# A graph layer with residual and norm on one core: x's three bf16 parts taken from its bytes, tables ahead of the edges' work, one set's picks by another queue

## The chip, the core and the metric

The kernel runs on one core of a Trainium2 chip: TensorE (PE) with its weight loads (PEld), VectorE (DVE), ScalarE (ACT), GpSimd (POOL), SyncE (SP), and sixteen DMA engines that they share. Each engine works through its own instructions in order; SP, ACT and POOL also issue DMAs from their queues. The metric is the device time of one execution in microseconds.

## The reference

Inputs are x (12500 x 128, float32), 400000 edges with source, target (sorted by target) and a type 0 or 1, and three 128 x 128 weights with biases.

```python
Xs = X[src]
m_data = Xs @ W_data.T + b_data
m_ctrl = Xs @ W_control.T + b_control
msg = jnp.where((edge_types == 0)[:, None], m_data, m_ctrl)
agg = jax.ops.segment_sum(msg, dst, num_segments=X.shape[0])
out = jax.nn.relu(agg + (X @ W_self.T + b_self))
x = _layernorm(x + out, axis=-1)          # mean and variance over the row, eps 1e-5
```

## The kernel before

**What is summed.** The kernel does not multiply each edge by a weight. It sums source rows per target and type, and multiplies the sums afterwards. The edges are cut into 25 groups of 125 columns of 128 edges. Of each group about a fifth comes by gathers from DRAM (`p`, GpSimd's indirect DMAs at L754) and the rest is picked from x in SBUF by TensorE (`e`, 107 sets of 20 columns, L820). Since TensorE works in bf16, x is held as three bf16 parts whose sum is x: `x3` in SBUF with 98 blocks of 128 rows, and `rows3`, the same in DRAM, for the gathers.

**The split of x** (`split_x`, L245). x is cut into eight pieces: six of 14 blocks, one of 13 and one of a single block with 84 rows. Four float32 tiles `xt` hold fetched pieces; a unit splits a piece and then issues the fetch of the piece four later into the tile that comes free (ACT's queue, L257). The split alternates two engines: ScalarE rounds x to bf16 (L262), VectorE subtracts it (L263), ScalarE rounds the rest (L264), VectorE subtracts that (L265). `store_rows` (L269) writes each piece's parts to `rows3` from SP's queue.

**A set of picked edges** (`give_slots`, L546). Each edge has a block of x (its source over 128) and a lane in it. Every one of 100 cells (blocks, two of them spare) has room for 32 edges of a set; VectorE and TensorE work out each edge's rank in its cell: `O` compares blocks with cells (L504), `prod` and `ahead` count (L576, L594, L598, L603 to L607), `eq` finds equal blocks in one lane (L565), `rm` and `rv` lay rank, lane and code out (L504, L635; `placed[0]` is the rv written down last). TensorE collects them (L647), ScalarE copies them to `cell` (L655), and two DMAs by SP's queue bring the lanes to all partitions: `there` in DRAM (L657) and from there `pick`, 800 KB (L659). VectorE compares `pick` with the partition's number (L690), and from then on TensorE can pick the set's rows out of `x3` (L820). ScalarE copies them to bf16 (`emsg`, L834), and TensorE adds them up with a 0/1 matrix of targets (`esel`, L504; L704 and L842). Edges beyond 32 in a cell are fetched by a spare gather (`last`, L798), used at the end of the set. `accumulate` adds the sums to `acc` (L743); finished rows are multiplied by the weights, added to x and normed.

**The opening.** Before the first set, the kernel loads the edges of group 0 and the first targets of all windows, makes tables (comparison columns, identity, `ltri`) from GpSimd's iotas (L304 to L345), works out each window's first node (`halves`, `node0`, L357 to L368), prepares group 0's edges (`prep_e`, L475: relative targets, codes, and copies of blocks, lanes and codes by ScalarE), splits x, ranks sets 0 and 1, and finds the windows' places (`places_and_weights`, L374, written down behind the third piece of x). Lines 1029 to 1047 give that order.

**What sets the order.** The instructions are written down in one order; for every engine a planner at build time makes a list from that order and its own estimate of when inputs are there. `merged` and `evenly` interleave units of work by a share of the set, and `paced` ties gathers to a point of TensorE's work. `tc.issue_after(ins)` queues the instructions of its block that run on `ins`'s engine behind `ins` on that engine; work of other engines in the block is not touched by it.

Of the kernel before, what the change touches and what calls it, by code (L numbers as in the profile page):

```python
# [10 lines left out]
I32 = mybir.dt.int32  # L11
AF = mybir.ActivationFunctionType
# [138 lines left out]
def short_path(ctx, tc, const, ident, eps, wT, brow, bad, x, src, dst, etype, ws, bs, out):  # L151
# [93 lines left out]
    def split_x(pool):  # L245
# [13 lines left out]
        def split(b, m, rows):  # L259
            t = tiles.pop(b)  # L260
            h, mm, lo = (x3[:rows, b:b + m, j, :] for j in range(3))
            nc.scalar.copy(h, t)  # L262
            nc.vector.tensor_sub(t, t, h)  # L263
            nc.scalar.copy(mm, t)  # L264
            parted.append(nc.vector.tensor_sub(lo, t, mm))  # L265
# [10 lines left out]
        for k, p in enumerate(pieces):  # L276
            def unit(k=k, p=p):
                split(*p)
                if k + ahead < len(pieces):
                    fetch(*pieces[k + ahead])  # L280
# [63 lines left out]
    for a in range(4):  # L344
        nc.vector.tensor_scalar(ltri[:, a, :], free[:, a, :], own_f[:, a:a + 1], None, op0=OP.is_gt)  # L345
# [10 lines left out]

    halves = tmp.tile([1, 2, NG * NE], I32, name="halves")  # L357
    nc.vector.memset(x3[:, NBLK - 1], 0.0)
    first = first_i["e"].rearrange("o g w -> o (g w)")
    nc.vector.tensor_single_scalar(halves[:, 0, :], first, 7, op=OP.logical_shift_right)  # L360
    nc.vector.tensor_single_scalar(halves[:, 1, :], first, 127, op=OP.bitwise_and)
# [12 lines left out]
    def places_and_weights():  # L374
        near = raw["near"] = keep.tile([rows_p, NG], FP, name="near")
        from_i = tmp.tile([rows_p, 1], I32, name="from_i")
        from_f = tmp.tile([rows_p, 1], FP, name="from_f")
        nc.gpsimd.iota(from_i, pattern=[[0, 1]], base=-PAD, channel_multiplier=DPC)
        nc.vector.tensor_copy(from_f, from_i)
        for k in range(1, NE):  # L380
            ge = raw[f"ge{k}"] = tmp.tile([rows_p, 1], FP, name=f"ge{k}")
            nc.vector.tensor_scalar(
                ge, from_f, float(DPC * PB * k - PAD), float(-DPC * PB), op0=OP.is_ge, op1=OP.mult
            )
        for k in range(1, NE):
            nc.vector.tensor_add(from_f, from_f, raw.pop(f"ge{k}"))
# [5 lines left out]
        least = tmp.tile([1, NG, NWIN], FP, name="least")  # L392
        for i, (_, _, c, _) in enumerate(windows(0)):
            nc.vector.memset(least[:, :, i:i + 1], float(max(0, c * DPC - PAD)))
# [80 lines left out]
    def prep_e(g):  # L475
# [17 lines left out]
        for v, val in enumerate((parts[:, 1, :], code)):  # L493
            nc.scalar.copy(vals2[:, :, v, :], val.rearrange("p (n o) -> p n o", o=1).to_broadcast([P, n, 2]))
# [551 lines left out]
    for u in prep_p(0):  # L1046
        u()
# [201 lines left out]
```

## Time and profile before

Three runs took 1756.07, 1758.43 and 1759.98 us; the median is 1758.43. The profiled execution took 1757.87 us, and its span, from the first instruction to the last, is 1756.1 us.

| stretch, us | length | PE busy | DVE busy | ACT busy | POOL busy | GB/s |
|---|---|---|---|---|---|---|
| 0 to 68 | 68 | 5.72 | 55.42 | 27.34 | 3.67 | 257 |
| 68 to 1700 | 1632 | 1563.90 | 1513.37 | 1169.52 | 1295.19 | 147 |
| 1700 to 1757 | 57 | 45.66 | 26.45 | 32.38 | 17.78 | 59 |

"Busy" leaves out waits and DMA issues. An engine's row in the profile names the line, the engine, the operation, what it writes from what it reads, how often, and in brackets how long the engine stood idle before it and what ended that wait. The mean granted clock of TensorE is 0.995.

### The profile page before, as it was taken

How to read it: one execution, taken by the hardware profiler on the slowest of the kernel's cores; microseconds unless marked ns; L12 is line 12 of the kernel's file. 1: busy time of each engine (PE TensorE's matmuls, PEld its weight loads, DVE VectorE, ACT ScalarE, POOL GpSimd, SP SyncE). 2: the span in 40 equal slices, each digit the busy share in tenths (PEclk: the TensorE clock that was granted, in tenths of full speed). 3: DMA queues.
4: the chain of work that ended last, by engine and by line, in shares of the span. 5: the costliest groups of instructions: out<-in, count | busy, mean ns of one | idle time of the engine just before them, and what ended most of it. 6: DMA issues, size and time to landing. Idle time of an engine off the chain costs nothing.

```text
span 1756.1 us, 72083 instructions
## 1 busy us (share of the span) xinstructions
PE 1615.3 (92%) x29945; PEld 1311.7 (75%) x29945; DVE 1595.2 (91%) x3996; ACT 1229.2 (70%) x2249; POOL 1316.6 (75%) x1109
## 2 busy tenths in 40 slices
PE   0599999999999999999999999999999989999997
PEld 0377777777778777777877877777777777878786
DVE  8899999998999998999988999999999989999993
ACT  4577777767677667767766777776777766767675
POOL 0288877787777787877887877887877877777871
PEclk9999999999999999999999999999999999999999
DMA  8655454446454545444535454544454535544441
GB/s 237 209 165 160 128 158 136 147 125 199 115 164 134 159 125 179 143 152 127 166 119 164 150 164 133 164 122 147 160 159 135 158 108 162 167 139 141 151 139 41
DMA packets 190562, 261.28 MB, mean 149 GB/s; under 512 B 86437, under 2 KB 155983, under 8 KB 187152
## 3 DMA queue, kind: packets, MB, share of 16 engines
q1 hardware_dynamic: 126894, 148.02, 25.9%
q0 software_dynamic: 50704, 102.16, 20.8%
q10 hardware_dynamic: 12626, 6.40, 1.2%
q8 instruction: 236, 3.87, 0.9%
q14 instruction: 102, 0.84, 0.1%
HBM read 238.47 MB, written 18.00 MB: 146 GB/s over the span
## 4 chain that ended last, share of the span: by engine, by line
PE 48%; DVE 32%; issue 6%; DMA 6%; ACT 5%; DVEq 1%; POOL 1%; SPq 0%; POOLq 0%; ACTq 0%
PE sums L704 22%; PE got L820 15%; DVE esel L504 3%; PE side L950 3%; DVE pick L690 3%; PE sums L842 3%; DMA last<-rows,idx 3%; DVE rv L635 2%; ACT emsg L834 2%; DVE prod L598 2%; DVE prod L576 2%; PE side L584 2%; DVE acc L743 2%; PE side L647 2%; DVE ahead L594 2%
## 5 line engine op out<-in xcount | busy, mean ns | idle before, releaser
L754 POOL DMA_INDIRECT msg<-rows,pidx x985 | 1190.9, 1209 | 307.5 <-issue 118.9
L834 ACT CAST emsg<-got 128x768 bf16<-128x768 f32 (+1 forms) x1070 | 951.9, 930 | 303.9 <-PE got L820 289.8
L704 PE MATMUL sums<-esel,emsg 128*128 128x176 bf16 x7704 | 683.4, 240 | 0.0
L704 PEld LDWEIGHTS <-emsg 128*128 128x128 bf16 x7704 | 566.9, 98 | 68.7 <-issue 28.5
L820 PE MATMUL got<-x,pick 128*32 128x384 bf16 x10486 | 568.0, 330 | 21.9 <-DVE pick L690 14.7
L820 PEld LDWEIGHTS <-pick 128*32 128x32 bf16 x10486 | 239.2, 96 | 139.2 <-issue 20.6
L504 DVE TENSOR_TENSOR esel<-code_col,code 128x1760 bf16<-128x1760 bf16 x321 | 292.7, 912 | 13.6 <-PE sums L704 11.6
L798 POOL DMA_INDIRECT last<-rows,idx x107 | 122.0, 1141 | 106.0 <-DVE pick L690 63.7
L704 PE MATMUL sums<-psel,msg 128*128 128x48 bf16 x2955 | 184.2, 184 | 17.2 <-DVE acc L743 15.2
L842 PE MATMUL sums<-esel,one_col 128*32 128x176 bf16 x2675 | 193.7, 240 | 4.4 <-DVE acc L743 4.4
L704 PEld LDWEIGHTS <-msg 128*128 128x128 bf16 x2955 | 149.9, 97 | 36.2 <-issue 31.4
L842 PEld LDWEIGHTS <-one_col 128*32 128x32 bf16 x2675 | 111.9, 97 | 60.7 <-issue 4.1
L790 PE MATMUL sums<-psel,one_col 128*128 128x48 bf16 x985 | 150.2, 183 | 0.0
L743 DVE TENSOR_TENSOR acc<-acc,sums 128x352 f32 (+2 forms) x232 | 99.4, 430 | 40.4 <-PE sums L704 36.8
L504 DVE TENSOR_TENSOR O<-cell_col,blk 128x2000 bf16<-128x2000 bf16 x107 | 128.2, 1198 | 2.1 <-issue 2.1
L598 DVE TENSOR_TENSOR prod<-O,ahead 128x2000 bf16<-128x2000 bf16 x107 | 127.6, 1193 | 0.1
L690 DVE TENSOR_SCALAR pick<-pick,lane_f 128x3200 bf16<-128x3200 bf16 x107 | 113.2, 1058 | 0.0
L647 PE MATMUL side<-rv,O 128*128 128x64 bf16 x2140 | 83.3, 195 | 31.6 <-DVE rv L635 30.6
L647 PEld LDWEIGHTS <-O 128*128 128x128 bf16 x2140 | 78.7, 100 | 33.3 <-DVE rv L635 29.3
L594 DVE TENSOR_REDUCE ahead<-side 128x100 bf16<-128x500 f32 x107 | 72.2, 675 | 28.0 <-PE side L520 27.3
L790 PEld LDWEIGHTS <-one_col 128*128 128x128 bf16 x985 | 94.3, 96 | 0.0
L635 DVE TENSOR_TENSOR rv<-rm,vals 128x1280 bf16<-128x1280 bf16 x107 | 87.8, 821 | 0.3
(170 smaller groups left out, 1869.2 us busy)
## 6 DMA issues: line engine op xcount, KB each, us to landing
pick<-there SPq DMA_DIRECT2D x107, 800.0 KB
acc<-acc_start SPq DMA_DIRECT2D x23, 1280.0 KB
msg<-rows,pidx POOLq DMA_INDIRECT x985
rows<-x SPq DMA_DIRECT2D x6, 1344.0 KB
xs<-in_x_dram SPq DMA_DIRECT2D x99, 62.5 KB
out_dram<-h SPq DMA_DIRECT2D x99, 62.5 KB
xt<-in_x_dram ACTq DMA_DIRECT2D x6, 896.0 KB
there<-cell SPq DMA_DIRECT2D x107, 6.2 KB
```

Source lines behind the costliest of these rows:

```text
L504: nc.vector.tensor_tensor(sel.rearrange("p n (w t) -> p n w t", t=2), col[:rows].rearrange("p (o w t) -> p o w t", o=1, t=2).to_broadcast( ...
L598: nc.vector.tensor_tensor(prod, s["O"], ahead.rearrange("p (o j) -> p o j", o=1).to_broadcast([P, EC, NCELL]), op=OP.mult)
L635: placed[:] = [nc.vector.tensor_tensor(rv.rearrange("p c v (r t) -> p c v r t", t=2), rm.rearrange("p c (o r t) -> p c o r t", o=1, t=2).t ...
L647: nc.tensor.matmul(s["rk"][:m, :2 * CAP], s["held"][:, c * NCELL:c * NCELL + m], s["rv"][:, c].rearrange("p v r -> p (v r)"), start=(c == ...
L690: nc.vector.tensor_scalar(t, t, lane_f, None, op0=OP.is_equal)
L704: last = nc.tensor.matmul(out, msg[:, j * D:(j + 1) * D], sel, start=(start and j == 0), stop=stop, skip_group_check=True)
L743: added.append(nc.vector.tensor_add(win, win, ps[:, :4 * wide].rearrange("p (a w) -> p a w", w=wide)[:, :, :width]))
L754: return nc.gpsimd.indirect_dma_start(out=msg, out_offset=None, in_=rows3[:, :], in_offset=bass.IndirectOffsetOnAxis(ap=codes["p", g][0][: ...
L790: nc.tensor.matmul(cnt, one_col, sel, start=False, stop=(c == n - 1), skip_group_check=True)
L820: last = nc.tensor.matmul(ps[CAP * a:CAP * (a + 1), :], slots[w]["pick"][:, a * NQ + q, :], x3[:, 4 * q + a - a0].rearrange("p j d -> p (j ...
L834: nc.scalar.copy(msg[:, :n], ps[:, :n, :3 * D])
L842: nc.tensor.matmul(cells_of(s["ps"], EW, 1)[CAP * (q % 4):CAP * (q % 4 + 1), :], one_col[:, :CAP], s["sel"][q], start=(q < 4), stop=(q + 4 ...
```

## The change

Four things are edited.

1. *The split.* No float subtraction is left. The upper two bytes of a float32 are a bf16 number: ScalarE copies them as the first part. The two lower bytes are read as whole numbers 0 to 255, and ScalarE writes them as bf16, scaled by 2^-15 and 2^-23, into the second and third part. VectorE masks the first part's mantissa off (sign and exponent stay, in a new tile `power`, as int16) and multiplies the two other parts by it. A piece takes three instructions of ScalarE and two of VectorE. ScalarE's part is queued behind `ready`, the last copy of a value in `prep_e(0)`.
2. *Order in the opening.* `halves` and the VectorE part of `prep_e(0)` are queued behind the last table (`ltri`), `prep_e(0)` is written down ahead of the first piece of x, and `from_f`, its steps and `least` move from `places_and_weights` to the place ahead of `halves`.
3. *Order behind sets.* The VectorE part of `prep_p(0)` is queued behind set 1's rv, and that of every later `prep_e` behind the rv written down last.
4. *Queue.* For set 0 alone `there` and `pick` are issued by GpSimd's queue in place of SP's.

```diff
         def split(b, m, rows):
             t = tiles.pop(b)
-            h, mm, lo = (x3[:rows, b:b + m, j, :] for j in range(3))
-            nc.scalar.copy(h, t)
-            nc.vector.tensor_sub(t, t, h)
-            nc.scalar.copy(mm, t)
-            parted.append(nc.vector.tensor_sub(lo, t, mm))
+            part = x3[:rows, b:b + m]
+            byte = t.bitcast(U8).rearrange("p k (d b) -> p k d b", b=4)
+            nc.scalar.copy(part[:, :, 0, :], t.bitcast(BF).rearrange("p k (d b) -> p k d b", b=2)[:, :, :, 1])
+            for j in range(2):
+                nc.scalar.activation(part[:, :, 2 - j, :], byte[:, :, :, j], AF.Copy, scale=2.0 ** (8 * j - 23))
+            power = pool.tile([P, step, D], BF, name="power", bufs=2)[:rows, :m, :]
+            nc.vector.tensor_single_scalar(
+                power.bitcast(I16), part[:, :, 0, :].bitcast(I16), -128, op=OP.bitwise_and
+            )
+            parted.append(nc.vector.tensor_tensor(
+                part[:, :, 1:, :], part[:, :, 1:, :],
+                power.rearrange("p k (j d) -> p k j d", j=1).to_broadcast([rows, m, 2, D]), op=OP.mult,
+            ))
...
             def unit(k=k, p=p):
-                split(*p)
+                with tc.issue_after(ready.ins):
+                    split(*p)
...
     for a in range(4):
-        nc.vector.tensor_scalar(ltri[:, a, :], free[:, a, :], own_f[:, a:a + 1], None, op0=OP.is_gt)
+        tables = nc.vector.tensor_scalar(ltri[:, a, :], free[:, a, :], own_f[:, a:a + 1], None, op0=OP.is_gt)
...
+    from_i = tmp.tile([rows_p, 1], I32, name="from_i")
+    from_f = tmp.tile([rows_p, 1], FP, name="from_f")
+    nc.gpsimd.iota(from_i, pattern=[[0, 1]], base=-PAD, channel_multiplier=DPC)
+    nc.vector.tensor_copy(from_f, from_i)
+    steps = {}
+    for k in range(1, NE):
+        steps[k] = tmp.tile([rows_p, 1], FP, name=f"ge{k}")
+        nc.vector.tensor_scalar(
+            steps[k], from_f, float(DPC * PB * k - PAD), float(-DPC * PB), op0=OP.is_ge, op1=OP.mult
+        )
+    for k in range(1, NE):
+        nc.vector.tensor_add(from_f, from_f, steps[k])
+    least = tmp.tile([1, NG, NWIN], FP, name="least")
+    for i, (_, _, c, _) in enumerate(windows(0)):
+        nc.vector.memset(least[:, :, i:i + 1], float(max(0, c * DPC - PAD)))
...
-    nc.vector.tensor_single_scalar(halves[:, 0, :], first, 7, op=OP.logical_shift_right)
-    nc.vector.tensor_single_scalar(halves[:, 1, :], first, 127, op=OP.bitwise_and)
+    with tc.issue_after(tables.ins):
+        nc.vector.tensor_single_scalar(halves[:, 0, :], first, 7, op=OP.logical_shift_right)
+        nc.vector.tensor_single_scalar(halves[:, 1, :], first, 127, op=OP.bitwise_and)
...
-            nc.scalar.copy(vals2[:, :, v, :], val.rearrange("p (n o) -> p n o", o=1).to_broadcast([P, n, 2]))
+            last = nc.scalar.copy(vals2[:, :, v, :], val.rearrange("p (n o) -> p n o", o=1).to_broadcast([P, n, 2]))
         codes["e", g] = (blk, twice("blk2", parts[:, 0, :]), vals2, pk)
+        return last
...
-            nc.sync.dma_start(out=there[:, :], in_=cell[:NCELL, :CAP])
+            queue = nc.sync if w else nc.gpsimd
+            queue.dma_start(out=there[:, :], in_=cell[:NCELL, :CAP])
             pick = s["pick"] = two.tile([P, NCELL, CAP], BF, name="pick")
-            nc.sync.dma_start(
+            queue.dma_start(
...
+    with tc.issue_after(tables.ins):
+        ready = prep_e(0)
     split_units.pop(0)()
-    prep_e(0)
...
-    load(1, "e")
-    load(1, "p")
-    for u in prep_p(0):
-        u()
+    with tc.issue_after(placed[0].ins):
+        load(1, "e")
+        load(1, "p")
+        for u in prep_p(0):
+            u()
...
+    def later(g):
+        with tc.issue_after(placed[0].ins):
+            prep_e(g)
...
-            more.append((0.1, lambda: prep_e(g + 1)))
+            more.append((0.1, lambda: later(g + 1)))
```

(The same lines for `from_i`, `from_f`, the steps and `least` leave `places_and_weights`.)

16 lines of the change are left out of this document (2 added, 14 removed).

## The prediction

> **What bounds the kernel now.** I read the page first, then the busy time by stretch, then the chain of waits of the opening.
>
> ```profile
> span 1756.1 us, 72083 instructions
> ...
> PE 1615.3 (92%) x29945; PEld 1311.7 (75%) x29945; DVE 1595.2 (91%) x3996; ACT 1229.2 (70%) x2249; POOL 1316.6 (75%) x1109
> ```
>
> Busy time by stretch (after the stretch and its length: busy time of PE, weight loads, DVE, ACT and POOL, the granted clock, the DMA share, GB/s):
>
> ```profile
> 0.00:68.00 68.00, 5.72 (x71) 4.36 (x71) 55.42 (x142) 27.34 (x31) 3.67 (x17) 1.00 0.86 257
> 68.00:1700.00 1632.00, 1563.90 (x29139) 1270.50 (x29143) 1513.37 (x3771) 1169.52 (x2158) 1295.19 (x1076) 1.00 0.48 147
> ```
>
> There are two stages. From 68 us to 1700 TensorE is busy 1563.90 of 1632 us and bounds the kernel, with VectorE close behind. Up to 68 us TensorE does 5.72 us of work: that is an opening in which x is split, sets 0 and 1 are ranked and set 0's picks come back. Nearly all of the change lies in it. So the question is by how much TensorE's first pick comes earlier, and whether the 1688 us behind it move along.
>
> The chain of waits through the opening (start, length, what):
>
> ```profile
> 38.09 8.06 DMA rows<-x
> ...
> 46.22 4.11 DMA xt<-in_x_dram
> ...
> 59.77 0.12 DVE ge L382 x2
> ...
> 61.87 0.73 DVE rv L635
> ...
> 62.98 0.05 DVE from_f L386
> ...
> 63.47 0.26 DVE least L394 x6
> ...
> 66.98 0.97 DVE pick L690
> ...
> 68.00 1.82 PE got L820 x19
> ```
>
> TensorE starts at 68.00 because VectorE compares set 0's picks (L690) at 66.98, and that instruction is queued behind both sets' ranking (rv, L635) and the split's subtractions. VectorE is busy 55.42 of those 68 us, and its idle time has three large pieces, one ahead of the edges' work (first row) and two by its waits (total, times, longest):
>
> ```profile
> 9.04 0.22 DVE L360 TENSOR_SCALAR halves<-first_e 1x125 int32<-1x125 int32 x1 [6.03 <-DMA edst<-in_dst_dram]
> ```
>
> ```profile
> DVE xt L263 <- ACT x L262: 2.7, 1, 2.7
> DVE x L265 <- ACT x L264: 2.5, 1, 2.5
> ```
>
> The first wait ends at 9.04, when the edges' destinations have landed. After it VectorE works 66.98 - 9.04 = 57.9 us with 5.2 us of holes, so the opening is VectorE's list of work, and I keep a ledger of that list.
>
> **The change part by part.**
>
> *The split on VectorE.* Old: two float subtractions a piece. New: one mask over 1792 two-byte numbers and one product over 3584. The rows (mean ns behind the busy time):
>
> ```profile
> L263 DVE TENSOR_TENSOR xt<-xt,x 128x1792 f32<-128x1792 f32 x6 | 12.1, 2014 | 0.0
> L265 DVE TENSOR_TENSOR x<-xt,x 128x1792 bf16<-128x1792 f32 x6 | 12.1, 2014 | 2.5 <-ACT x L264 2.5
> L598 DVE TENSOR_TENSOR prod<-O,ahead 128x2000 bf16<-128x2000 bf16 x107 | 127.6, 1193 | 0.1
> L603 DVE TENSOR_TENSOR prod<-prod 128x1000 bf16<-128x1000 bf16 x107 | 72.5, 678 | 2.0
> L690 DVE TENSOR_SCALAR pick<-pick,lane_f 128x3200 bf16<-128x3200 bf16 x107 | 113.2, 1058 | 0.0
> L526 DVE TENSOR_SCALAR om_all<-slot_col,side 128x448 bf16<-128x448 bf16 x107 | 38.8, 362 | 0.0
> ```
>
> L598 is a bf16 product with one operand repeated over the middle dimension, the form of the new one: from L603 to L598 it is 0.515 ns an element, so 1.193 + 1584 x 0.515 ns = 2.01 us. The mask has no row of its own, for no two-byte integer appears. Bounds: 0.70 us by L526 and L690 (0.253 ns an element, 0.362 + 1344 x 0.253 ns), 2.01 us by the subtractions (one element a cycle). I take 0.70, because the form, one two-byte input in SBUF and a constant, is that of L690. A piece then costs 2.71 instead of 4.03 us, and the eight pieces, which make 7.0 full ones, 19.0 instead of 28.2: 9.2 us off the list.
>
> *Tables ahead of the edges' work.* VectorE runs them between these starts:
>
> ```profile
> 11.38 0.20 DVE L305 CAST cell_col<-i 128x100 bf16<-128x100 int32 x1
> ...
> 13.30 0.25 DVE L444 SCALAR_TENSOR_TENSOR ecode<-erel,esec 128x100 f32<-128x100 f32 x1
> 13.48 0.87 DVE L345 TENSOR_SCALAR ltri<-i,own_f 128x128 bf16<-128x128 int32 x4
> 14.26 0.25 DVE L491 SCALAR_TENSOR_TENSOR pk<-esrc,ecode 128x100 f32<-128x100 int32 x1
> ```
>
> That is 13.30 - 11.38 plus 14.26 - 13.48 = 2.7 us, which go into the 6.0 us hole that ends at 9.04. Cover is left: if the tables ran late there, whatever passes 6.0 us would delay set 0 one for one.
>
> *from_f, its four steps and least* leave the end of the list for the same hole: 4 comparisons at 0.06, 4 additions at 0.05 and 10 memsets at 0.26/6 us, together 0.9 us. With the tables that is 3.6 us in a hole of 6.0.
>
> *The split on ScalarE* grows from two to three instructions a piece. Rows:
>
> ```profile
> 10.71 1.28 ACT L262 ACT_TABLE_LOAD   x1 [10.71 <-DMA etyp<-in_edge_type_dram]
> ...
> 14.03 0.35 ACT L494 CAST vals<-ecode 128x200 bf16<-128x200 f32 x1
> ...
> 18.07 1.68 ACT L262 CAST x<-xt 128x1792 bf16<-128x1792 f32 x1
> 19.66 1.68 ACT L264 CAST x<-xt 128x1792 bf16<-128x1792 f32 x1
> ...
> 46.85 1.58 ACT L262 CAST x<-xt 128x1664 bf16<-128x1664 f32 x1 [7.52 <-DMA rows<-x]
> ...
> 50.56 0.20 ACT L655 CAST cell<-side 128x64 bf16<-128x64 f32 x1
> ```
>
> Back to back a cast takes 19.66 - 18.07 = 1.59 us. Byte reads with a stride have no row; bounds 1.59 and, at half the rate, 3.2; I take 1.59, as 1792 elements are 1792 elements in both reads. Three a piece make 4.77, seven pieces 33.4 us. They are now queued behind prep_e(0)'s copies, which end near 12.9 (the table load ends at 11.99, three small casts follow). With 1.5 us for the small copies of sets 0 and 1, ScalarE is through at 47.8 and VectorE's mask and product of the last two pieces at about 50.5. That is below VectorE's own end, found next, so these 10 us more of ScalarE are hidden with a cover of 3.7 us; past that cover they count. In exchange ScalarE no longer waits for VectorE between its casts, and x's tiles are free once ScalarE has read them, so a fetch no longer stands behind a subtraction.
>
> *Set 0's picks by GpSimd's queue.* Today both copies stand on SP, between other loads and stores:
>
> ```profile
> 50.78 0.30 SPq L657 DMA_DIRECT2D there<-cell  x1
> ...
> 54.55 0.36 SPq L659 DMA_DIRECT2D pick<-there  x1
> ```
>
> From the cell copy at 50.56 to the compare at 66.98 are 16.4 us, an upper bound for the two transfers. In the new order ScalarE reaches the cell copy behind four pieces, 12.9 + 4 x 4.77 = 32 us, or 34 with a wait; 34 + 16.4 = 50.4 is before VectorE is ready. So I cost it at nothing. SP loses two issues, which takes nothing from what stands behind them, and GpSimd has no work then (POOL 3.67 us up to 68).
>
> *Waits added.* Splits behind the last copy of prep_e(0): priced in the 12.9 us. prep_p(0) behind set 1's rv: it runs later than that today. prep_e of later groups behind rv of a set whose rank has been written down before: eight small VectorE instructions a group, which can only be kept from running early; nothing on TensorE, bounded by plus or minus 0.1 us a set below.
>
> *Sum.* 9.2 + 2.7 + 0.9 = 12.8 us off VectorE's list: compare at 54.2, first pick at 55.2. What TensorE needs soon after must be there too: the last pieces of x by 50.5, and the rows for the spare gather.
>
> ```profile
> 15.00:20.00 5.00, 0.00 (x0) 0.00 (x0) 5.00 (x4) 4.75 (x4) 0.00 (x0) 1.00 0.40 79
> ...
> 30.00:35.00 5.00, 0.00 (x0) 0.00 (x0) 5.00 (x5) 2.59 (x2) 0.00 (x0) 1.00 1.12 357
> ```
>
> GpSimd's and TensorE's lists:
>
> ```profile
> 68.07 2.96 POOL L798 DMA_INDIRECT last<-rows,idx  x1 [63.74 <-DVE pick L690]
> ...
> 86.51 0.39 PE L704 MATMUL sums<-esel,last 128*128 128x176 bf16 x3
> ```
>
> The gather of set 0 starts at 68.07 and is used at 86.51, 18.5 us after the first pick; moved along, that use stands at 73.7. Even if the stores kept it until 68.07 + 2.96 = 71.0 it would be in time. So all 12.8 us reach the end: 1757.87 - 12.8 = 1745.1 for the profiled execution, whose time is 0.56 below the median shown (1758.43). I forecast 1745. Of the 5.2 us of holes I count none as gained; if all closed it would be 1740.
>
> **The rivals.** Within 0.2% (3.5 us, about what a measurement of this kernel can tell from no change) lies between 1754.9 and 1761.9.
>
> 1. *ScalarE's queue takes over.* It runs in order, and the row at 46.85 shows it standing 7.52 us because a fetch ahead of it waited for a store. One such wait in the new list puts the last product at 58.0, 3.8 past 54.2: 1749; two would eat nearly everything: 1756.5. For it: the DMA share of 1.12 once stores run. Against: only 0.40 at 15 to 20 us, where the fetches now go out. Chance 0.16.
>
> 2. *VectorE's new instructions run at one element a cycle: slower.* By L263 (2.014 us for 1792, 1.04 ns an element) the product would take 3.88 and the mask 2.01: 5.89 a piece instead of 4.03, 13.0 us more, less the 3.6 of the tables: 1767. It turns slower from 4.54 us a piece. For it: no row shows the mask, and the outputs are strided. Against: L598. Chance 0.06. The mask alone at that rate gives 4.02 a piece, no gain from the split, 1754.3: 0.07.
>
> 3. *The change works, but the rest is ordered anew and loses it.* TensorE has 68.1 us of holes in its 1632. A shift of 0.1 us in each of the 107 sets is 10.7: 1756 (0.07), or 1734 the other way (0.05).
>
> 4. *Set 0's picks come late from GpSimd, and the move does not free anything.* What GpSimd's issues can take shows here:
>
> ```profile
> L754 POOL DMA_INDIRECT msg<-rows,pidx x19: 942/1006/4798, 73.2 to 109.8; - x19
> ```
>
> Two issues at the longest, 4.8 us, add 9.6 to 50.4: compare at 60.0, 1751. If they stood until VectorE's list is done and the transfers came only then, 54.2 + 16.4 = 70.6: 1761.5. Chance 0.02. The Trainium skill, SBUF — State Buffer, section "SBUF: two separate sides", speaks for this rival: VectorE's two-port modes lock GpSimd out while it writes descriptors, and the page advises SP's or ScalarE's queue. By that rule the new masks would hold the picks up for some of their length each; the 4.8 us row may be such a case, but the median of 1.0 beside a VectorE that is 93% busy says that a lockout is short.
>
> **How the numbers follow.** The forecast has 0.57 (its own range 1739 to 1750). Faster: 0.57, 0.12 of rival 1, 0.05 of the masked case, 0.07 of rival 3, together 0.81. Slower: 0.06 of rival 2, 0.01 each of rivals 3 and 4, 0.08. Same: 0.11. From 1737 to 1756 leaves out the good end of rival 3 (0.05) above all, rival 2 and half of the bad ends (0.15).
>
> **What would show it.** The first pick near 55; tables done before 9; the mask at 0.7 and the product at 2.0 us; ScalarE without waits on VectorE between its casts; picks issued by POOL near 34; the spare gather near 60; the stretch behind the first pick as long as before. I would be wrong if ScalarE stands behind fetches, if the product takes 3.9, or if that stretch has grown.

## The result, and the profile after

The changed kernel takes 1757.67 us (median of 14 runs, 1751.45 to 1762.45), the kernel before, run beside it, 1757.12: a ratio of 1.0006, with a 95% interval from 0.9992 to 1.0021. The forecast was 1745, 0.7% faster. There is no difference that these runs can tell from none.

The profiled execution of the changed kernel, span and busy times from its page:

```profile
span 1754.3 us, 72075 instructions
...
PE 1619.0 (92%) x29945; PEld 1311.7 (75%) x29945; DVE 1587.5 (90%) x3996; ACT 1235.4 (70%) x2257; POOL 1305.5 (74%) x1111
```

Its busy time by stretch, with the columns of the table before (PE, weight loads, DVE, ACT, POOL, granted clock, DMA share, GB/s):

```profile
0.00:68.00 68.00, 11.82 (x129) 6.91 (x130) 54.09 (x154) 42.81 (x46) 5.08 (x19) 1.00 0.87 256
68.00:1700.00 1632.00, 1562.48 (x29099) 1268.61 (x29098) 1507.93 (x3760) 1161.20 (x2153) 1283.61 (x1076) 0.99 0.48 147
```

TensorE does 11.82 us of work in the first 68 us where it did 5.72, so the start is earlier. ScalarE is busy for 42.81 us of them instead of 27.34. VectorE's 54.09 us (before 55.42) hold some 8 us behind its compare, which now comes earlier; up to the compare, from the first landed edges on, its busy time compares like this (columns as above), first of the kernel before, then of the changed one:

```profile
9.04:66.98 57.94, 5.72 (x69) 4.26 (x68) 52.30 (x128) 27.34 (x31) 0.00 (x0) 1.00 0.88 268
```

```profile
9.07:58.88 49.81, 4.35 (x55) 3.39 (x54) 39.06 (x80) 36.49 (x32) 1.40 (x2) 1.00 0.85 251
```

VectorE's work is 13.2 us less, and its holes grew from 5.6 us (57.94 less 52.30) to 10.8 (49.81 less 39.06). What the new instructions cost, on VectorE and on ScalarE:

```profile
6.00 0.87 DVE L356 TENSOR_SCALAR ltri<-i,own_f 128x128 bf16<-128x128 int32 x4
9.07 0.21 DVE L387 TENSOR_SCALAR halves<-first_e 1x125 int32<-1x125 int32 x1 [1.95 <-DMA edst<-in_dst_dram]
15.33 0.62 DVE L269 TENSOR_SCALAR power<-x 128x1792 int16<-128x1792 int16 x1
19.12 2.02 DVE L272 TENSOR_TENSOR x<-x,power 128x3584 bf16<-128x3584 bf16 x1
29.14 0.35 DVE L431 CAST part<-brow 1x384 bf16<-1x384 f32 x1 [6.87 <-DMA brow<-in_L_gnn_b_self_dram]
```

```profile
14.79 3.28 ACT L267 ACTIVATE x<-xt 128x1792 bf16<-128x1792 uint8 x2
23.90 3.28 ACT L267 ACTIVATE x<-xt 128x1792 bf16<-128x1792 uint8 x2 [4.26 <-DMA ptyp<-in_edge_type_dram]
37.50 0.21 ACT L643 CAST bits_b<-bits 128x24 bf16<-128x24 int32 x1 [4.94 <-DVE bits L641]
```

The sizes of the new instructions came out as forecast, and the tables fill the hole ahead of 9.07 (1.95 us are left of 6.03). Three new stops stand in the lists: VectorE waits 6.87 us for a bias row, because `bparts` now comes this early in its list, and ScalarE waits 4.26 us behind a fetch and 4.94 us for a value of VectorE.

TensorE starts 8.0 us earlier (59.97, before 68.00), and then stops in set 1. Its rows:

```profile
59.97 1.46 PE L835 MATMUL got<-x,pick 128*32 128x384 bf16 x13 [2.62 <-DVE pick L705]
...
103.27 0.33 PE L719 MATMUL sums<-esel,last 128*128 128x176 bf16 x1 [8.87 <-DMA last<-rows,idx]
103.53 1.79 PE L835 MATMUL got<-x,pick 128*32 128x384 bf16 x20
```

It waits 8.87 us for the spare gather of set 1. That one is GpSimd's, in order behind ten others:

```profile
73.38 0.97 POOL L813 DMA_INDIRECT last<-rows,idx  x1 [24.60 <-DMA ptyp<-in_edge_type_dram]
74.66 1.09 POOL L769 DMA_INDIRECT msg<-rows,pidx  x1 [0.31 <-ACT emsg L849]
76.05 4.27 POOL L769 DMA_INDIRECT msg<-rows,pidx  x1 [0.30 <-PE got L835]
...
84.42 4.36 POOL L769 DMA_INDIRECT msg<-rows,pidx  x1 [0.30 <-issue]
...
91.70 5.83 POOL L769 DMA_INDIRECT msg<-rows,pidx  x1 [0.30 <-issue]
97.83 0.91 POOL L813 DMA_INDIRECT last<-rows,idx  x1 [0.30 <-issue]
```

The first spare gather comes at 73.38, 5.3 us later than before (68.07), for all of x must be stored, and the split now ends at 63.4 where it ended at 60.4 (3.0 of the 5.3); three of the nine gathers behind it take 4.3 to 5.8 us in place of 1. Behind the stop TensorE runs slowly (windows, columns as above):

```profile
100.00:103.00 3.00, 0.00 (x0) 0.00 (x0) 0.00 (x0) 0.00 (x0) 2.09 (x3) 0.50 0.78 181
...
107.00:109.00 2.00, 2.00 (x28) 1.17 (x29) 0.18 (x1) 1.54 (x4) 1.53 (x2) 0.50 0.32 81
109.00:111.00 2.00, 2.00 (x32) 1.74 (x33) 1.61 (x3) 0.68 (x1) 1.10 (x2) 0.84 0.17 38
111.00:113.00 2.00, 2.00 (x43) 1.68 (x35) 1.68 (x5) 1.81 (x2) 1.70 (x2) 1.00 0.06 14
```

The granted clock is 0.50 until about 109.7. Where the gain went can be read from VectorE's additions of the edge sums into the set's accumulator, which close a set. Sets 0 and 3 of the changed kernel, and of the kernel before:

```profile
80.52 0.52 DVE L758 TENSOR_TENSOR acc<-acc,sums 128x352 f32 x1 [0.31 <-PE sums L719]
...
136.71 0.50 DVE L758 TENSOR_TENSOR acc<-acc,sums 128x352 f32 x1
```

```profile
87.26 0.50 DVE L743 TENSOR_TENSOR acc<-acc,sums 128x352 f32 x1
...
131.16 0.51 DVE L743 TENSOR_TENSOR acc<-acc,sums 128x352 f32 x1
```

Set 0 closes 6.7 us earlier, set 3 closes 5.6 us later: 12.3 us are lost between them. The wait is 8.87 of it, and some 6 us of TensorE's work at half clock are worth about 3 more (an estimate). From there to the end the difference wanders between +5.6 and -7.4 us and ends at -1.0.

Over the whole span TensorE waits for spare gathers no longer than before. These rows (total, times, longest) are of the kernel before and of the changed one:

```profile
PE sums L704 <- DMA last<-rows,idx: 15.2, 11, 4.5
```

```profile
PE sums L719 <- DMA last<-rows,idx: 15.0, 3, 8.9
```

So the stop in set 1 tells where the lead of the start went, and not by itself why the total came out the same: the kernel before waits about as long, in smaller pieces and later.

### The profile page after: what moved, and what is told of

Read it like the earlier page. It is cut to its first block, busy times and chain, and to the rows that moved or that the text cites. A ratio compares the mean times of both kernels' runs of the same rounds, so it can differ in the third digit from the quotient of the medians.

```text
span 1754.3 us, 72075 instructions
## 1 busy us (share of the span) xinstructions
PE 1619.0 (92%) x29945; PEld 1311.7 (75%) x29945; DVE 1587.5 (90%) x3996; ACT 1235.4 (70%) x2257; POOL 1305.5 (74%) x1111
## 4 chain that ended last, share of the span: by engine, by line
PE 53%; DVE 28%; ACT 7%; issue 5%; DMA 3%; DVEq 1%; POOL 0%; ACTq 0%; SPq 0%; POOLq 0%
PE sums L719 24%; PE got L835 17%; PE side L965 4%; ACT emsg L849 4%; DVE esel L518 3%; DVE pick L705 3%; PE sums L857 3%; DVE rv L649 2%; DVE prod L612 2%; PE side L661 2%; PE side L598 2%; DVE prod L590 2%; DVE ahead L608 1%; ACT h L995 1%; DVE acc L758 1%
## 5 line engine op out<-in xcount | busy, mean ns | idle before, releaser
L813 POOL DMA_INDIRECT last<-rows,idx x107 | 113.6, 1062 | 74.0 <-DMA ptyp<-in_edge_type_dram 24.6
```

## The experiments

The theory after the first look: the gain is given back by GpSimd's list of gathers, which starts when the last rows are stored and not when TensorE starts. The rivals: the new order behind the sets (part 3) costs time by itself; the queue of set 0's picks does; nothing was won that could be lost, and the rest is scatter.

The kernels of the table are edits of the changed kernel or of the one before. For each, from its trace: TensorE's first pick, the issue of set 0's spare gather, the end of set 1's on GpSimd, "lag" from the first pick to that end, gathers over 2.5 us among those from the one spare to the other, TensorE's longest wait for a spare gather in the first three sets, and how much later than before set 3 closes. Times in us.

| kernel | first pick | spare 0 | spare 1 made | lag | long gathers | wait | set 3 | ratio to before, interval |
|---|---|---|---|---|---|---|---|---|
| before | 68.00 | 68.07 | 90.74 | 22.7 | 2.96 | 0 | 0 | 1 |
| changed | 59.97 | 73.38 | 98.74 | 38.8 | 4.27, 4.36, 5.83 | 8.87 | +5.6 | 1.0006 [0.9992, 1.0021] |
| e13, the same again | 60.23 | 73.72 | 99.77 | 39.5 | 5.34, 4.35, 5.20 | 9.00 | +4.5 | 1.0014 [0.9995, 1.0032] |
| e5, later() undone | 61.21 | 74.70 | 95.42 | 34.2 | 4.95, 2.89 | 4.66 | +0.2 | 1.0006 [0.9985, 1.0027] |
| e1, spare first | 59.84 | 73.28 | 87.57 | 27.7 | 4.32, 4.32 | 7.16 | +2.4 | 1.0010 [0.9988, 1.0032] |
| e14, parts of e9 and e2 | 65.39 | 75.08 | 96.10 | 30.7 | 5.86 | 5.84 | +2.6 | 0.9993 [0.9978, 1.0007] |
| e2, bparts late | 58.22 | 72.16 | 92.54 | 34.3 | 5.02 | 2.62 | -3.5 | 0.9981 [0.9963, 0.9999] |
| e6, picks by SP | 59.61 | 71.98 | 91.81 | 32.2 | 4.35 | 0 | -6.3 | 0.9985 [0.9971, 0.9998] |
| e9, part 3 undone | 61.52 | 74.22 | 90.95 | 29.4 | none | 0.92 | -6.3 | 0.9980 [0.9959, 1.0001] |
| e4, split alone | 61.55 | 73.85 | 92.52 | 31.0 | 4.35 | 1.03 | -4.8 | 0.9969 [0.9948, 0.9991] |
| e12, split and queue | 61.47 | 73.76 | 91.95 | 30.5 | 4.35 | 0 | -5.2 | 0.9979 [0.9959, 1.0000] |
| e3, old split | 64.69 | 66.94 | 88.72 | 24.0 | none | 0 | -2.0 | 1.0029 [1.0005, 1.0053] |
| e11, last rows stored twice | 68.24 | 80.38 | 100.83 | 32.6 | 2.83 | 0.19 | +1.7 | 1.0052 [1.0029, 1.0074] |

**Only the split (e4_split_alone), and the change without it (e3_old_split).** The split of the one kernel is put into the other, nothing else.

```diff
-            h, mm, lo = (x3[:rows, b:b + m, j, :] for j in range(3))
...
+            nc.scalar.copy(part[:, :, 0, :], t.bitcast(BF).rearrange("p k (d b) -> p k d b", b=2)[:, :, :, 1])
...
```

> The kernel before with the new split alone: old order, old queue. By the ledger (9.2 us of VectorE) the first pick comes near 59 to 60. Theory S: the last piece of x is ready no earlier than before (60.4), and the first pick comes at 62 to 68. By theory Q the total gains whatever of the earlier start is not lost again to the spare gather of set 1: near the time before, within 5 us.

> The changed kernel with the old split (two casts, two float subtractions a piece) and everything else changed. By my ledger the split took 9.2 us off VectorE's list, so the first pick should come at 66 to 69. Theory S (ScalarE carries the new split): in the changed kernel the last piece of x is ready at 63.4, later than the 60.4 of before, because ScalarE has three casts a piece and stands 9 us in between; with the old split the last piece is then ready at or before 61, and the first pick at 60 to 64.

First picks, of e4 and of e3:

```profile
61.55 0.50 PE L830 MATMUL got<-x,pick 128*32 128x384 bf16 x1
```

```profile
64.69 2.56 PE L827 MATMUL got<-x,pick 128*32 128x384 bf16 x28 [0.66 <-DVE pick L697]
```

Alone, the split brings the first pick from 68.00 to 61.55; the rest of the change, without it, to 64.69. Together they give 59.97. So 6.5 and 3.3 us add up to 8.0 and not to 9.8. The split alone was the fastest version of its comparison: TensorE waits 1.0 us in set 1, and sets 0 to 18 close 3.4 to 5.3 us earlier than before. At set 19 that lead is gone in the profiled execution (0.1 us), which was the slowest of its ten. Without the split the last piece of x is ready at 59.8 (before 60.4), and the spare gathers are early (66.94); no wait above 1 us stands in the first three sets. Yet this version measured 0.3% slower, and what costs that is not settled: its sets 0 to 3 close 2.0 to 3.4 us early, set 4 closes 3.0 late.

**Spare gathers ahead of the others (e1_spare_first).** Four gathers stand between the first two spares in place of nine.

```diff
-    due[:] = [(LAG - 0.1) * (k + 0.5) / AHEAD for k in range(AHEAD)] + due[:-AHEAD]
+    due[:] = [0.2 * (k + 0.5) for k in range(4)] + [1.35 + 0.055 * k for k in range(AHEAD - 4)] + due[:-AHEAD]
```

> The changed kernel, with only four of the fourteen early gathers due in set 0 and the others due from the middle of set 1, so that on GpSimd's in-order list set 1's spare gather stands behind four gathers instead of nine. Theory Q (queue): the changed kernel wins 8.0 us at the first pick (59.97 against 68.00) and loses them in set 1, where TensorE stands 8.9 us for that spare gather and then runs at half the granted clock for some 9 us. By it the spare gather is issued near 82 instead of 97.8, the wait in set 1 is under 2 us, set 1's sums are added near 95 instead of 105.8, no stretch is at a clock of 0.5, and the total is 8 to 12 us below the changed kernel, near 1747. Rival R (reordering): what the opening wins is taken back by the anew ordered sets behind it; then set 1 ends earlier too, but the total stays within 3 us of the changed kernel. Third possibility: too few gathers are ahead when set 2 begins, and the wait moves to set 2.

The wait in set 1 is gone and another one stands in set 2:

```profile
116.35 0.62 PE L719 MATMUL sums<-esel,last 128*128 128x176 bf16 x3 [7.16 <-DMA last<-rows,idx]
```

A gather moved ahead makes another one late: it is the list as a whole that is behind, not one place in it. The time is that of the changed kernel.

**Part 3: one half of it (e5_no_later), all of it (e9_no_part3).** `prep_e` of later groups no longer waits for the rv; in e9 `prep_p(0)` does not either.

```diff
-            more.append((0.1, lambda: later(g + 1)))
+            more.append((0.1, lambda: prep_e(g + 1)))
```

> The changed kernel without the queueing of later prep_e behind the last rv. Theory Q: first pick at 60 and the 8.9 us wait in set 1 as in the changed kernel, total within 3 us of it. Rival R: if the order behind the opening is what costs, the total is at least 5 us lower, near 1750, while the opening is the same.

> The changed kernel with its part 3 (order behind sets) undone: preparation of group 0's targets and of later groups without the wait for the rv. Theory: it is not among the causes; first pick 59 to 62, spare gather of set 0 at 73 to 75, a wait of 4 to 10 us in set 1 or 2, ratio to before 0.998 to 1.003. If part 3 is what takes away the gain that the split alone has (0.9969), the ratio is 0.994 to 0.998 and the wait in set 1 is below 2 us.

With e5 the wait stays, at about half (4.66 us) with two long gathers instead of three; the time does not move. With e9 the first pick comes 1.5 us later than in the changed kernel, no long gather falls between the spares, and the wait is gone, from the view of waits and GpSimd's rows:

```profile
PE sums L719 <- DMA last<-rows,idx: 0.9, 1, 0.9
```

```profile
74.22 1.20 POOL L813 DMA_INDIRECT last<-rows,idx  x1 [25.40 <-DMA ptyp<-in_edge_type_dram]
...
89.70 1.25 POOL L813 DMA_INDIRECT last<-rows,idx  x1 [0.30 <-issue]
```

From one spare to the other it takes 15.5 us (89.70 less 74.22) where the changed kernel takes 24.5 (97.83 less 73.38), for the same nine gathers between. I had expected part 3 to be no cause; of the wait it is one. In the time the intervals of e9 and of the changed kernel overlap. How part 3 does it is not shown. It is not by filling VectorE's holes, for between the spares of e9 VectorE has almost none (third number behind the length, 16.61 of 16.73 us), where in the changed kernel it is busy 22.13 of 25.36:

```profile
74.22:90.95 16.73, 15.85 (x286) 12.05 (x286) 16.61 (x44) 15.80 (x31) 13.68 (x11) 1.00 0.59 176
```

**bparts behind the last table of set 0 (e2_bparts_late), and together with e9 (e14_no_part3_bparts_late).**

```diff
-    bparts()
+    with tc.issue_after(placed[0].ins):
+        bparts()
```

> The changed kernel with VectorE's work of bparts queued behind the last table of set 0, so that the hole of 6.87 us before L431 is filled. If that hole and the holes of 4.26 and 4.94 us on ScalarE that follow it are what cost the missing 4.8 us of the start, TensorE's first pick comes at 54 to 57 us in place of 59.97. If ScalarE's three casts a piece set the end by themselves, it stays at 59 to 61. Either way the theory that GpSimd's gathers take over expects no gain at the end: the first spare gather stays near 73, a wait of 7 to 12 us in set 1 or 2, ratio 0.998 to 1.003.

> The changed kernel with part 3 undone and bparts' VectorE work behind the last table, the two edits that each gave 0.998. If the two gains are separate, first pick at 56 to 59, no wait above 3 us in sets 0 to 2, ratio 0.995 to 0.998. If GpSimd's gathers bound the first sets whatever the first pick's time, the second edit adds nothing: ratio 0.997 to 1.000.

Filling the hole of 6.87 us brings the first pick only 1.75 us forward: ScalarE's three instructions a piece set the end, as the second case of the expectation had it. With one long gather between the spares instead of three, the waits are down to 2.6 us in set 0 and 1.8 in set 1, and the time to 0.9981. The two edits together do not add up. The list falls differently again: the first pick at 65.39, the spare of set 1 itself a gather of 5.86 us, a wait of 5.84 us, and a ratio of 0.9993.

**The queue: back to SP (e6_sp_queue), and added to the split alone (e12_split_queue).**

```diff
-            queue = nc.sync if w else nc.gpsimd
+            queue = nc.sync
```

> The changed kernel with set 0's cells and picks back on SP's queue. The prediction costed the queue at nothing. If that holds, first pick at 59 to 62 and the ratio to before 0.999 to 1.002, as of the changed kernel. If the queue matters, the picks wait behind SP's transfers and the first pick comes after 63, or the spare gather of set 0, no longer behind two issues on GpSimd, comes before 72.

> The kernel before with the new split and set 0's picks by GpSimd's queue, and nothing else of the change. The split alone gave 0.9969 with a first pick at 61.55. If the queue is what loses that gain, a wait of 4 to 9 us for a spare gather stands in set 1 or 2 and the ratio is 0.999 to 1.003. If the queue does nothing (or the picks simply come when the cells are there), the first pick is at 60 to 62 and the ratio 0.995 to 0.998.

In both pairs the first pick is the same to 0.4 us (59.61 and 59.97, 61.55 and 61.47), so the queue is worth nothing to the start, as forecast. Its removal, though, brings the first spare gather 1.4 us forward and leaves one long gather instead of three; in the first three sets no wait for a spare gather is left (0.55 us in the next one). Added to the split alone the queue costs nothing that shows: as there, nine gathers with one long one (4.35 us) stand between the two spares, and TensorE does not wait.

**The same kernel again (e13_after_again).**

> The changed kernel itself once more, unedited: a second profiled execution of the same program. If the wait of 8.87 us for the spare gather of set 1 belongs to the program (the order of GpSimd's list and the late rows), it stands here again with 6 to 10 us. If it comes from long gathers that fall differently in each execution, the gathers between 74 and 98 take another time than 23 us, the wait is another one or gone, and set 3 ends up to 8 us earlier or as late. First pick in both cases within 1 us of 59.97; ratio 0.998 to 1.002.

```profile
103.17 0.33 PE L719 MATMUL sums<-esel,last 128*128 128x176 bf16 x1 [9.00 <-DMA last<-rows,idx]
```

A second execution shows the same wait and three long gathers at nearly the same places (74.99, 84.59 and 92.12). The stop belongs to the program; it is not scatter.

**Late gathers by themselves (e11_stored_twice).** The kernel before, its last three pieces of x stored twice.

```diff
-            for b, m, rows in pieces:
+            for b, m, rows in pieces + pieces[-3:]:
```

> The kernel before, with the last three pieces of x stored twice (some 2.6 MB more, about 8 us at the rate of the stores): its first pick stays at 68, the spare gather of set 0 comes 5 to 9 us later than 68.07 and all gathers behind it. It prices late gathers by themselves. Theory (gathers of the first sets bound them): TensorE waits 4 to 9 us for a spare gather in set 0, 1 or 2, the sets behind it end 4 to 9 us later, ratio 1.001 to 1.005. Rival (the gathers have room): no wait above 2 us, the first five sets within 2 us of before, ratio 0.999 to 1.001.

Its first spare gather comes 12.3 us later, more than the 5 to 9 expected, and it is 0.5% slower by the ratio (the medians differ by 6.9 us), with TensorE's first pick where it was. The mechanism is the expected one, the place is not: the first three sets wait for nothing (0.19 us), set 4 does, and set 9 again:

```profile
PE sums L704 <- DMA last<-rows,idx: 9.2, 4, 5.2
```

So the list of gathers, once late, stays behind for sets, and TensorE pays where its lead runs out. That is the clearest sign that the rows' time, and not only the first pick's, bears on the time of this kernel.

**What makes a gather long (m1_gathers_alone, m2_pauses).** The whole computation is left out; what is left is ten gathers of 128 rows by GpSimd beside one kind of work, in stages.

```diff
+    stages = [(None, 0), (tt, 44), (ts, 70), (sc, 24), (ff, 40), (small, 220)]
...
+                g = nc.gpsimd.indirect_dma_start(
```

> Leaves the whole computation out (the output holds gathered rows of x): six stages of ten gathers of 128 rows each by GpSimd, alone, beside VectorE's bf16 products of 128x2000 back to back, beside its bf16 products with a constant, beside ScalarE's copies, beside float32 products of 128x1000, and beside very short products. If VectorE's work keeps GpSimd from making a gather, a gather takes 0.9 to 1.1 us alone and beside ScalarE, and 2 to 6 us beside back-to-back work of VectorE in at least one form. If long gathers come from the DMA queues or the rows' addresses, all stages show the same 0.9 to 1.3 us.

> Leaves the whole computation out. Six stages of ten gathers: alone, beside VectorE's unbroken bf16 products of 128x1000, of 128x400, of 128x1600, beside sums over 128x500 float32, and beside runs of five bf16 products with a constant (128x2000, about 3 us) broken by one that waits for ScalarE. If a gather is finished only in a pause of VectorE, or in the pause between two long products, it takes about 1.9 us beside products of 128x1600, much longer beside 128x400, and in the last stage every gather ends at a pause, 3 to 4.5 us apart. If only the instruction's form counts and not the pauses, the last stage shows one gather as long as the whole stage (over 30 us).

GpSimd's rows of the first: alone, beside long bf16 products, beside bf16 products with a constant (two rows), and beside ScalarE:

```profile
14.10 0.95 POOL L106 DMA_INDIRECT got<-in_x_dram,idx  x1 [0.30 <-issue]
...
30.29 1.92 POOL L106 DMA_INDIRECT got<-in_x_dram,idx  x1 [0.30 <-issue]
...
76.66 41.23 POOL L106 DMA_INDIRECT got<-in_x_dram,idx  x1 [26.69 <-DVE c L82]
118.20 0.95 POOL L106 DMA_INDIRECT got<-in_x_dram,idx  x1 [0.31 <-issue]
...
135.43 0.95 POOL L106 DMA_INDIRECT got<-in_x_dram,idx  x1 [0.30 <-issue]
```

One gather stood 41.23 us, until VectorE had done all 70 products; the next took 0.95. The second kernel: beside products of 128x1000, of 128x400 (two rows), and beside runs of five products with a constant broken by a pause (two rows); then VectorE's row at the first pause:

```profile
29.24 1.47 POOL L108 DMA_INDIRECT got<-in_x_dram,idx  x1 [0.30 <-issue]
...
56.97 25.21 POOL L108 DMA_INDIRECT got<-in_x_dram,idx  x1 [12.11 <-DVE c L80]
82.48 0.94 POOL L108 DMA_INDIRECT got<-in_x_dram,idx  x1 [0.30 <-issue]
...
164.79 2.91 POOL L108 DMA_INDIRECT got<-in_x_dram,idx  x1 [16.85 <-DVE c L88]
168.00 1.01 POOL L108 DMA_INDIRECT got<-in_x_dram,idx  x1 [0.30 <-issue]
```

```profile
167.22 0.19 DVE L87 TENSOR_SCALAR c<-d 128x100 bf16<-128x100 bf16 x1 [0.34 <-ACT d L86]
```

What comes out: ten gathers take 0.94 to 0.95 us each alone (a first one 1.08), beside ScalarE, and beside VectorE's sums; 1.46 to 1.50 beside bf16 products of 128x1000 and 128x1600 back to back; 1.91 to 1.92 beside those of 128x2000 and beside float32 ones (the first of each of these four stages 1.13 to 1.66). And beside unbroken runs of products with a constant, of products of 128x400 or of 128x100, the first gather stands for as long as the run lasts (41.23, 25.21 and 27.01 us). With a pause of 0.34 us that ends at 167.22, the gather that stood ends at 164.79 + 2.91 = 167.70. Of the two cases expected for this last stage neither came: after the first pause the further gathers pass at 1.0 us, with the products stretched to 3.50 us for five where they had taken 3.03. So here a pause let a gather through that was shut out; what decides whether the next is shut out again stays open. From VectorE's last instruction, or from the start of the pause, to the gather's end it took 0.8 us each time (117.07 to 117.89, and 166.89 to 167.70).

The three long gathers of the changed kernel end near holes of VectorE, too. The first long gather ends at 76.05 + 4.27 = 80.32, and VectorE, without a hole from 75.1 on, stands for 0.31 us ahead of the addition at 80.52 shown above. The second ends at 88.78, and VectorE rests from 88.35 to 89.46:

```profile
87.98 0.37 DVE L619 TENSOR_TENSOR prod<-prod,eq 128x400 bf16<-128x400 bf16 x1
89.46 0.22 DVE L474 CAST psf<-psrc 45x128 f32<-45x128 int32 x1 [1.11 <-issue]
```

The third ends at 97.53, after VectorE's last instruction ahead of its own long stop (96.85 and 0.15 long). But they end only 0.11, 0.43 and 0.53 us behind the start of the hole, where it took 0.8 above, and the rest of the run does not bear such a rule out. Of the 26 gathers over 2.5 us in the changed kernel, the other 23 run and end beside a VectorE that has no hole over 0.05 us: from 1157.80 to 1161.34, for one of 3.54 us, it is busy all the time. The kernel before has 26 such gathers as well. That VectorE's work can shut a gather out is shown by the two kernels without the computation; what makes a gather long in the whole kernel, and what ends it, is not.

**A pause put in (g1_gap, r4_gap), and the candidates side by side (r1_split_alone_again, r2_split_alone, r3_no_part3).** The picks of sets 1 to 3 take their lane numbers from a copy that ScalarE makes.

```diff
+                with tc.issue_after(placed[0].ins):
+                    stop = nc.vector.tensor_copy(one, lane_f)
+                nc.scalar.copy(lane, one)
...
-                nc.vector.tensor_scalar(t, t, lane_f, None, op0=OP.is_equal)
+                nc.vector.tensor_scalar(t, t, lane, None, op0=OP.is_equal)
```

> The changed kernel in which the picks of sets 1 to 3 (L705) take their lane numbers from a copy that ScalarE makes of a copy of VectorE, so that VectorE may have to pause ahead of each of these picks until ScalarE has got to it. If pauses of VectorE let gathers through, the nine gathers behind the first spare take less than 23 us (15 to 20), the spare of set 1 is issued at 90 to 95, TensorE's wait for it falls from 8.9 to below 6 us. If ScalarE gets to the copy before the list reaches the pick there is no pause, the gathers stay at 22 to 25 us and the wait at 8 to 10. Ratio 0.996 to 1.002 in both cases.

> The changed kernel with the pause ahead of the picks of sets 1 to 3 once more. On a chip of the usual time, if pauses let gathers through: the spare of set 1 issued at 90 to 95, TensorE's wait for it 0 to 5 us in place of 8.9, ratio 0.997 to 1.000. If not: gathers as in the changed kernel, a wait of 8 to 10 us, ratio 1.000 to 1.002.

> The kernel before with the new split alone, unedited from the earlier run, in five rounds. If its gain is real the ratio is 0.996 to 0.998 with an interval below 1; if the earlier 0.9969 was scatter, 0.999 to 1.001. First pick at 61 to 62 again, and no wait above 2 us in set 1, if its gathers fall as before.

> The split alone once more. If its gain of the start stays to the end: ratio 0.996 to 0.998, interval below 1. If the rest of the run wanders by as much as the start gains: 0.998 to 1.001.

> The change without part 3 once more. First pick 61 to 62, no wait above 2 us for a spare gather in sets 0 to 2; ratio 0.996 to 0.999 if the gain stays, 0.999 to 1.001 if not.

These five ran on chips on which the kernel before takes 2074 us and TensorE often stands with no cause that the profile shows, so they are compared only with it. The ratios: pause 0.9981 [0.9957, 1.0006] and 0.9991 [0.9973, 1.0009], part 3 undone 0.9992 [0.9975, 1.0008], split alone 1.0008 [0.9984, 1.0033] and 1.0016 [0.9993, 1.0039]. In both runs with the pause no wait for a spare gather is left in the first sets. In the first of them the pause does not end the gather that stands there: it lasts from 78.88 to 79.15, and the gather, 4.54 us long, from 75.78 to 80.32. In the second, VectorE and GpSimd at the pause:

```profile
81.14 1.05 DVE L711 TENSOR_SCALAR pick<-pick,lane 128x3200 bf16<-128x3200 bf16 x1 [0.69 <-ACT lane L709]
```

```profile
78.27 3.01 POOL L775 DMA_INDIRECT msg<-rows,pidx  x1 [0.30 <-PE got L841]
```

The gather ends at 81.28, just behind the pause from 80.45 to 81.14. So the two disagree on whether the pause let the gather through. Set 1 closes at 107.95 and 106.30 there, no earlier than in the changed kernel on the other chips (105.77), for TensorE then stands for other things (in the first run 5.3 us for ScalarE's copies). And as the changed kernel without the pause was not run on such a chip, neither the mechanism nor a gain is shown by these runs. The 0.9969 of the split alone does not carry over to these chips, and none of the versions is shown to beat both kernels everywhere.

## Why the prediction was wrong

*Right.* The ledger of VectorE's list was right: 13.2 us came off it (12.8 forecast). So were the sizes on VectorE: mask 0.62 us (0.70 forecast), product 2.02 (2.01), tables in the hole ahead of 9.07. Rival 2 is out with these rows. The picks' queue is worth nothing to the first pick: 59.61 without it, 59.97 with it. Only the time of its issues was wrong, 43.26 for 34, as ScalarE reaches the cells later:

```profile
43.26 0.78 POOL L672 DMA_DIRECT2D there<-cell  x1 [38.93 <-ACT cell L669]
```

*"The split on ScalarE" was mis-sized.* A byte activation takes 1.6 us as forecast, but ScalarE was to be through at 47.8 and VectorE's last product to end at 50.5; the last product ends at 63.4. The sum of 33.4 us was right and the cover was not: the list runs in order, and stops of 4.26 and 4.94 us stand in it. (The "10 us more" of ScalarE are 11.1 by the prediction's own row, seven pieces of 1.59 us; nothing hangs on it.) I had named a stop behind a fetch as rival 1, with a chance of 0.16. VectorE's holes, which the sum left at 5.2 us, grew by 5.1, and the start comes 4.8 us later than forecast (first pick 59.97, forecast 55.2). The largest hole in the changed kernel is the 6.87 us for the bias row, by the order of VectorE's own list; with that wait gone (e2) VectorE waits 6.2 us for ScalarE's split instead (4.3 and 1.9), and only 1.75 us are won back. By itself the later start would have left 1757.87 - 8.0 = 1749.9. That this is close to the 1749 of rival 1 is in part luck, for only one of ScalarE's two stops is of its kind.

*"Sum" failed: "Even if the stores kept it until 71.0 it would be in time. So all 12.8 us reach the end."* I looked at the spare gather of set 0 alone, and at its use; I expected it near 60, and it came at 73.38. The gather of set 1 stands nine gathers behind it, and its cover was nowhere worked out. In the kernel before it is made 22.7 us behind the first pick; the kernels with a lag of 29 to 33 wait 0 to 1.03 us, those with 34.2, 38.8 and 39.5 wait 4.66, 8.87 and 9.00. (Two do not fit this measure. e2, at 34.3, waits 1.80 us in set 1, having waited 2.62 in set 0. e14, at 30.7, waits 5.84: its set 0 closes nearly as early as the others' in spite of its late first pick.) So there were some 7 us of cover. An earlier first pick (8.0), a later first spare (5.3) and slower gathers (2.7) took 16.0 of it: 22.7 + 16.0 is the 38.8 of the changed kernel, to rounding. (The 2.7 is what is left of the long gathers: the nine between the spares take 10.9 us more than before, but GpSimd stands idle 5.2 us less between them, and the two spares themselves take 3.0 less.) Each microsecond by which TensorE alone was moved ahead was to be paid from that cover, and the split's later end paid from it too.

*The size of the stop* comes from long gathers. Three of them are 14.5 us where three at 0.95 would be 2.9, that is 11.6 us more than without. This was in the prediction as rival 4, for two issues at the opening, with the Trainium skill's rule (SBUF — State Buffer, section "SBUF: two separate sides") beside it that VectorE's two-port modes shut GpSimd out while it writes descriptors. I put it aside there because the median gather took 1.0 us: "a lockout is short". The kernels without the computation bear the rule out for products with a constant, show that a lockout can last through a whole run of instructions (41.23 us), and show one beside short products of two tensors as well. That the three long gathers of the changed kernel are such lockouts is likely and not shown. They struck the gathers behind the picks, not the picks.

*Rival 3* named a loss in the rest. Part 3 does order VectorE's work anew in the stretch of the first gathers, and undoing it takes the wait away; but the loss shows as one stop in set 1, not as 0.1 us in each set. Behind set 3 the difference from the kernel before wanders between +5.6 and -7.4 us and ends at -1.0; beyond the late spare gathers that e11 shows, what makes it wander was not settled.

*The sign that the prediction named*, a longer stretch behind the first pick, came: from there to the end of the span it is 1694.3 us where it was 1688.1. Of these 6.2 us TensorE's busy time is 5.1 (1614.66 and 1609.57 us, with 14 products more), its holes 1.1.

*What stays open.* The changed kernel without its long gathers could not be run by itself: every edit that took two or all of them away (e2, e6, e9) also moved other work. And how much of the gain the stop cost is open: with the wait gone, e9 and e6 close set 3 by 6.3 us earlier than the kernel before and 11.9 earlier than the changed one, yet they are only 0.20% and 0.15% (2.6 to 3.5 us) faster than the kernel before. And e3, with no wait to show, is 0.3% slower for a reason not found.

## What to carry to other kernels

When an opening is shortened, look up for every engine that feeds the loop what starts its list: here TensorE starts with the picks, GpSimd with the last stored row, and what moves one alone can be lost to the other. Work out the cover of the second and third use of a list run in order, not of the first. A gather issued by GpSimd can stand while VectorE works, so look at the gathers' lengths again behind every change of VectorE's order.

## What the runs showed that was not expected

A gather by GpSimd stood 41 us beside an unbroken run of VectorE's bf16 products with a constant, and 25 and 27 us beside short products of two tensors, while long products of two tensors only stretched it from 0.95 to 1.5 or 1.9 us. The Trainium skill (SBUF — State Buffer, section "SBUF: two separate sides") has the lock held "for the whole instruction"; here it passed a gather over through 70 instructions.

After some 9 us without work TensorE's granted clock was 0.50 and stayed there for about 6 us of work (windows from 100 to 111): twenty picks took 1.79 us. By the estimate above this stop cost about a third more than its length. The Trainium skill (TensorE: Matmul & The Clock Gate, "Part 1: The HAM clock gate") tells of a half clock after an idle window and gives some 3.4 us of work until it is lifted; the trace agrees on the half and shows a longer return.

On two chips the kernel before took 2074 us, 18% more than on the others. The split alone there, from the view of waits:

```profile
PE got L830 <- issue: 55.2, 164, 1.1
PE sums L714 <- issue: 44.2, 126, 1.8
```

TensorE stands for nothing that the profile shows; on the other chips no such row is among the first seven of that kernel. The cause is open.
